# Deformable-convolution samples blended and scaled in their gather buffers instead of small buffers of their own

## The chip, the cores and the metric

The kernel runs on one core of a Trainium2 chip. The metric is the device time of one execution in microseconds (us), as the median of several executions of the same program. Five engines work beside each other, each through its own instructions in a fixed order: TensorE (PE; its weight loads are listed as PEld), VectorE (DVE), ScalarE (ACT), GpSimd (POOL), which here issues indirect DMAs, and SyncE (SP), which issues plain DMAs. They wait for each other through semaphores.

## The reference

One metaformer layer on `x` of shape 4 x 256 x 64 x 64 (images, channels, rows, columns), all in fp32. First three modulated deformable 3x3 convolutions, each followed by a ReLU, on the input normalised over channels; the result is added to `x`. Then a mixture of 8 experts (256 to 512 to 256, exact GELU), of which each position uses its best two, added again. The part that the change touches is the sampling of a deformable convolution:

```python
om = conv3x3(x, w_off) + b_off            # 27 channels: 9 offsets (dy, dx), 9 masks
ys = row + ky - 1 + dy                    # sampling place of each of the 9 taps
xs = col + kx - 1 + dx
sampled = bilinear(x, ys, xs) * sigmoid(mask)   # four neighbours, weighted
out = einsum('bikhw,oik->bohw', sampled, w) + b
```

## The kernel before

A layer of one image is a stage; there are 12 stages (3 layers, 4 images), ordered so that images interleave. A stage has 8 blocks of 512 positions (8 image rows), a block has 9 taps, and a tap has 4 tiles of 128 positions. One such tile of one tap is called a sample here: 128 positions x 256 channels. There are 12 x 8 x 9 x 4 = 3456 samples, handled in 1728 pairs.

The layer's input lies in HBM as a table whose rows hold a position and the one below it; two table rows that follow each other are two columns of the image. So one indirect DMA on POOL (L503) brings for each of 128 positions all four neighbours: 4 KB a partition, 512 KB in all, into a buffer `g` of the pool `gat`, which has `GB = 10` buffers (L38, L147). Then for each sample:

- L509, the column blend, on VectorE: in both columns the lower neighbour times its coefficient plus the upper, in place in `g` (512 elements a partition);
- L514, the row blend, on VectorE: the right column's result times its coefficient plus the left one's, into a small buffer `s` of the pool `smp` with 8 buffers (256 elements a partition);
- L517, the scaling by mask and weights, on ScalarE, in place in `s`.

`turn` handles a pair, two pairs behind the newest (`LAG = 2`): four 128x128 transposes on TensorE (L532) into PSUM, and a copy on ScalarE (L535) into `sT`. When the four samples of a tap are there, `finish` multiplies the preceding tap's `sT` with the tap's weights (L555: four matmuls of 128x512, each shown as two records) into the accumulator of the block; after nine taps ScalarE adds the bias and applies the ReLU (L577).

Other work is woven in, spread over the taps by the program: the offset convolution (L357) and sampling plan (L366 to L427) of coming blocks, the transposes and normalisation of coming images (L442 to L467), the storing of tables (L325 to L338), and the expert network of images that are done: its gathers on POOL (L800, L812, L915), matmuls on TensorE (L856, L874), GELUs on ScalarE (L866), and VectorE's bias and weighted sums (L892, L930). Expert gathers are queued behind the newest sample gather (`self.gathered`), and much of the VectorE work behind the newest row blend (`self.last`), with `self.after`, which fixes the order of issue on one engine and adds no wait.

The order in which each engine gets its instructions is set when the program is built, by a scheduler that works with its own estimates of durations and with the number of buffers in each pool; the chip then follows that order. A buffer that is handed on makes its next writer wait for the last reader of the old contents.

Of the kernel before, what the change touches and what calls it, by code (L numbers as in the profile page):

```python
# [8 lines left out]
F32 = mybir.dt.float32  # L9
I32 = mybir.dt.int32  # L10
AF = mybir.ActivationFunctionType
ALU = mybir.AluOpType
AX = mybir.AxisListType

P = 128
H = W = 64
C = 256
# [17 lines left out]
FT_LOG = 8  # L35
FT = 1 << FT_LOG
FU = FT // P
GB = 10  # L38
LAG = 2
LEAST = 2.0**-30  # L40
WINN = CC * (RPB + 2) * W
# [41 lines left out]
class Group:  # L83


    def __init__(self, b, n0, n1):
        self.b, self.n0, self.n1 = b, n0, n1
        self.nm = f"{b}_{n0}"
        self.M = (n1 - n0) * TPB

        self.NF = 2 * self.M * P // FT + E - 1


        self.half = (self.NF + 1) // 2
        self.zt, self.acc, self.gy, self.sums, self.py = {}, [], [], [], None
        self.order = [s // 2 + s % 2 * self.half for s in range(self.NF)]
# [21 lines left out]
class Weave:  # L118
# [3 lines left out]
    def __init__(self, ctx, tc, ins, out):  # L122
        nc = self.nc = tc.nc
        self.tc = tc
        self.ins = ins
        self.x = ins["x"].rearrange("b (c p) h w -> b p c (h w)", p=P)
        self.out_v = out.rearrange("b (c p) h w -> b p c (h w)", p=P)
        self.B = self.x.shape[0]

        def pool(name, bufs, **kw):  # L130
            return ctx.enter_context(tc.tile_pool(name=name, bufs=bufs, **kw))

        self.cst = pool("cst", 1)
        self.dram = pool("dram", 1, space=bass.MemoryType.DRAM)
        self.wkp = pool("wkp", 1)
        self.plan = pool("plan", 19)
        self.win = pool("win", 3)
        self.wt = pool("wt", 2)
        self.small = pool("small", 1)
        self.big = pool("big", 2)  # L140
        self.ffn = pool("ffn", 2)
        self.rt = pool("rt", 1)
        self.rt2 = pool("rt2", 2)
        self.gyp = pool("gyp", 4)
        self.smT = pool("smT", 2)
        self.smp = pool("smp", 8)
        self.gat = pool("gat", GB)  # L147
        self.ps = pool("ps", 3, space=bass.MemoryType.PSUM)
        self.ps1 = pool("ps1", 1, space=bass.MemoryType.PSUM)

        self.routes, self.tiles, self.sums = Lane(), Lane(), Lane()
        self.side, self.plans_side = [], []
        self.last = self.gathered = self.turned = None
        self.starting, self.draining, self.later = True, False, []
        self.pend, self.pairs = None, []
# [338 lines left out]
    def samples(self, i, n, k, t0, plan):  # L494


        nc = self.nc
        idx, cf = plan
        ss = []
        for t in (t0, t0 + 1):  # L500
            j = t * K + k
            g = self.gat.tile([P, 2, 2, C], F32, tag="g", name=f"g_{i}_{n}_{j}")
            self.gathered = nc.gpsimd.indirect_dma_start(  # L503
                out=g.rearrange("p x s f -> p (x s f)"),
                out_offset=None,
                in_=self.table(*self.stages[i]),
                in_offset=bass.IndirectOffsetOnAxis(ap=idx[:, j : j + 1], axis=0),
            )
            nc.vector.scalar_tensor_tensor(  # L509
                g[:, :, 0, :], g[:, :, 1, :], cf[:, j, 0:1], g[:, :, 0, :],  # L510
                ALU.mult, ALU.add,
            )
            s = self.smp.tile([P, C], F32, tag="s", name=f"s_{i}_{n}_{j}")
            self.last = nc.vector.scalar_tensor_tensor(  # L514
                s, g[:, 1, 0, :], cf[:, j, 1:2], g[:, 0, 0, :], ALU.mult, ALU.add
            )
            nc.scalar.activation(s, s, AF.Copy, scale=cf[:, j, 2:3])  # L517
            ss.append(s)
        return ss
# [616 lines left out]
```

## Time and profile before

| | |
|---|---|
| median of 9 runs | 7644.26 us (7624.54 to 7658.29) |
| profiled execution, its own time | 7608.72 us |
| its span, first to last instruction | 7607.0 us |
| mean granted TensorE clock | 0.94 |
| busy share of the span: TensorE, VectorE, ScalarE, POOL | 85%, 65%, 43%, 59% |
| DMA queue of the indirect gathers | 1947 MB, 72.5% of 16 DMA engines' span |
| 3456 gathers (L503) | 1069 ns each on POOL, 2435 us of POOL's idle time ahead of them |
| 3456 column blends (L509) | 743 ns each |
| 3456 row blends (L514) | 483 ns each |
| 3456 scalings (L517) | 508 ns each |
| 1728 copies of transposes (L535) | 586 ns each, 2409 us of ScalarE's idle time ahead of them |

In the profile's lists of groups a line has the source line, the engine, the operation, what is written and read with its shape, and the count; then, after a bar, the busy time in us and the mean of one instruction in ns; then, after a second bar, the engine's idle time just ahead of these instructions and what ended most of it. In the list of waits a line says who waited for whom: us in total, times, and the longest wait. "Issue" is time in which an engine waited for nothing that the profile shows, "remote" a wait whose end the profile could not attribute. In the timeline a line has the start and the duration in us, the engine, the line, the operation and the count, and in brackets the idle time ahead of it. Matmul ends are modelled in the records, so that TensorE's busy share isn't how close it is to its peak.

### The profile page before, as it was taken

The numbers are of one execution on the slowest core, as the hardware profiler recorded it, in microseconds if no ns is written. First come the engines' busy times: TensorE is split into PE (matmuls) and PEld (weight loads), VectorE is DVE, ScalarE is ACT, GpSimd is POOL, SyncE is SP. The second block draws the span as 40 slices with busy tenths as digits, with TensorE's granted clock in tenths as the row PEclk, the third lists the DMA queues.
The fourth block names the chain that finished last, engine by engine and source line by source line (L and its number), as shares of the span: only waits on it lengthen the run. The fifth ranks groups of instructions, "written<-read, shape, count | busy, mean of one in ns | idle before, by whom it ended". The sixth has DMA issues, their size and how long they took to land.

```text
span 7607.0 us, 88985 instructions
## 1 busy us (share of the span) xinstructions
PE 6459.0 (85%) x26500; PEld 3626.5 (48%) x26500; DVE 4952.9 (65%) x11467; ACT 3268.5 (43%) x7141; POOL 4485.9 (59%) x4245
## 2 busy tenths in 40 slices
PE   7897888888898888888987879988888788977887
PEld 3443333334444444455554445444444455644565
DVE  6776777768987666567777556656768454667421
ACT  3444444445544444445443434444444333444322
POOL 4654666656666556556557656655556565656543
PEclk8999999999999999999999989999999899999898
DMA  8997999989999888889888878888888777888644
GB/s 268 333 321 264 352 331 337 338 331 356 363 343 318 297 296 306 283 303 327 300 290 314 282 266 313 301 298 287 304 289 293 244 264 241 288 286 297 203 141 123
DMA packets 800319, 2223.73 MB, mean 292 GB/s; under 512 B 104728, under 2 KB 302872, under 8 KB 794080
## 3 DMA queue, kind: packets, MB, share of 16 engines
q0 software_dynamic: 551200, 1947.35, 72.5%
q1 hardware_dynamic: 248640, 270.69, 10.7%
q8 instruction: 215, 3.52, 0.2%
q14 instruction: 264, 2.16, 0.1%
HBM read 2160.68 MB, written 196.40 MB: 310 GB/s over the span
## 4 chain that ended last, share of the span: by engine, by line
PE 68%; ACT 10%; issue 8%; another core or an unknown queue 7%; DVE 4%; DMA 2%; POOL 1%; SPq 0%; ACTq 0%; POOLq 0%; DVEq 0%
PE acc L555 33%; PE tp L532 10%; PE ph L856 7%; PE py L874 7%; PE po L357 6%; ACT sT L535 3%; ACT s L517 3%; DVE g L509 1%; DVE s L514 1%; PE pm L371 1%; ACT hT L866 1%; ACT win L577 1%; PE ftp L840 1%; PE lp_tok L618 1%
## 5 line engine op out<-in xcount | busy, mean ns | idle before, releaser
L503 POOL DMA_INDIRECT g<-tab,idx x3456 | 3696.1, 1069 | 2435.4 <-DVE s L514 1095.6
L555 PE MATMUL acc<-sT,wk 128*128 128x512 f32 x6912 | 3501.5, 621 | 276.4 <-ACT sT L535 157.6
L509 DVE SCALAR_TENSOR_TENSOR g<-g,cf 128x512 f32<-128x512 f32 x3456 | 2560.8, 743 | 260.8 <-DMA g<-tab,idx 239.8
L514 DVE SCALAR_TENSOR_TENSOR s<-g,cf 128x256 f32<-128x256 f32 x3456 | 1663.2, 483 | 1394.2 <-PE tp L532 751.1
L535 ACT COPY sT<-tp 128x512 f32<-128x512 f32 x1728 | 1003.4, 586 | 2408.5 <-PE tp L532 1599.0
L555 PEld LDWEIGHTS acc<-sT,wk 128*128 128x128 f32 x6912 | 1201.3, 198 | 1128.5 <-issue 823.8
L517 ACT ACTIVATE s<-s,cf 128x256 f32<-128x256 f32 x3456 | 1631.1, 508 | 236.0 <-DVE s L514 145.0
L532 PEld LDWEIGHTS tp<-ident,s 128*128 128x128 f32 x6912 | 895.6, 146 | 1697.6 <-issue 999.9
L532 PE MATMUL tp<-ident,s 128*128 128x128 f32 x6912 | 1290.4, 287 | 461.5 <-ACT s L517 223.6
L856 PE MATMUL ph<-fzT,w 128*128 128x256 f32 x2608 | 720.3, 411 | 80.2 <-ACT fzT L844 30.1
L874 PE MATMUL py<-w,hT 128*128 128x256 f32 x2608 | 675.2, 397 | 120.1 <-ACT hT L866 66.2
L856 PEld LDWEIGHTS ph<-fzT,w 128*128 128x128 f32 x2608 | 507.1, 205 | 217.4 <-issue 80.1
L874 PEld LDWEIGHTS py<-w,hT 128*128 128x128 f32 x2608 | 485.5, 196 | 262.1 <-ACT hT L866 101.6
L866 ACT ACTIVATE hT<-ph,w 128x256 f32<-128x256 f32 x652 | 282.5, 472 | 619.2 <-PE ph L856 361.3
L812 POOL DMA_INDIRECT zt<-z,tok x326 | 335.3, 1028 | 159.5 <-issue 88.6
L800 POOL DMA_INDIRECT w<-in_W,wrow x163 | 176.2, 1081 | 400.3 <-ACT sT L535 163.3
L357 PE MATMUL po<-win,wo 128*32 128x504 f32 (+1 forms) x2304 | 364.3, 609 | 6.0 <-ACT win L301 3.6
L892 DVE TENSOR_TENSOR y<-py,w 128x512 f32<-128x512 f32 x163 | 111.9, 687 | 360.8 <-PE py L874 293.6
L915 POOL DMA_INDIRECT gy<-ys,slots x256 | 254.7, 995 | 104.8 <-issue 73.0
L930 DVE SCALAR_TENSOR_TENSOR ta<-gy,cw,ta 128x256 f32<-128x256 f32 x256 | 120.8, 481 | 121.3 <-DMA gy<-ys,slots 76.8
L357 PE MATMUL po<-win_pre,wo 128*32 128x504 f32 (+1 forms) x1152 | 185.7, 622 | 2.0 <-ACT om L366 2.0
L366 ACT ACTIVATE om<-po,bo 128x512 f32<-128x512 f32 x96 | 66.0, 688 | 247.1 <-PE po L357 155.9
(154 smaller groups left out, 2965.9 us busy)
## 6 DMA issues: line engine op xcount, KB each, us to landing
tab<-hv SPq DMA_DIRECT2D x512, 128.0 KB
g<-tab,idx POOLq DMA_INDIRECT x3456
ys<-y SPq DMA_DIRECT2D x163, 256.0 KB
tab<-h_pre SPq DMA_DIRECT2D x128, 256.0 KB
wk<-in_conv_w SPq DMA_DIRECT2D x99, 256.0 KB
xc_pre<-in_x SPq DMA_DIRECT2D x32, 512.0 KB
xr_tok<-in_x SPq DMA_DIRECT2D x32, 512.0 KB
t<-t_tok SPq DMA_DIRECT2D x32, 512.0 KB
```

What stands on the lines that cost most here:

```text
L357: nc.tensor.matmul(po[g * Q : (g + 1) * Q, :].rearrange("q (r w) -> q r w", w=W)[:, :, x0:x1], lhsT=self.wo[l][:, 3 * ky + kx, c, :], rhs= ...
L503: self.gathered = nc.gpsimd.indirect_dma_start(out=g.rearrange("p x s f -> p (x s f)"), out_offset=None, in_=self.table(*self.stages[i]), ...
L509: nc.vector.scalar_tensor_tensor(g[:, :, 0, :], g[:, :, 1, :], cf[:, j, 0:1], g[:, :, 0, :], ALU.mult, ALU.add,)
L514: self.last = nc.vector.scalar_tensor_tensor(s, g[:, 1, 0, :], cf[:, j, 1:2], g[:, 0, 0, :], ALU.mult, ALU.add)
L517: nc.scalar.activation(s, s, AF.Copy, scale=cf[:, j, 2:3])
L532: self.turned = nc.tensor.transpose(tp[:, c, u * P : (u + 1) * P], ss[u][:, c * P : (c + 1) * P], self.ident)
L535: nc.scalar.copy(self.sT[:, :, t0 * P : (t0 + 2) * P], tp)
L555: nc.tensor.matmul(acc[:, o, :], lhsT=self.wk[k][:, c, o * P : (o + 1) * P], rhs=sT[:, c, :], start=(k == 0 and c == 0), stop=(k == K - 1 ...
L812: self.nc.gpsimd.indirect_dma_start(out=zt, out_offset=None, in_=grp.zd, in_offset=bass.IndirectOffsetOnAxis(ap=grp.tok[:, j : j + 1], axi ...
L856: nc.tensor.matmul(ph[:, h, :], lhsT=w1[:, o : o + P], rhs=zT[:, c, :], start=(c == 0), stop=(c == CC - 1),)
L866: nc.scalar.activation(ht[:, h, :], ph[:, h, :], AF.Gelu, bias=w1[:, k : k + 1])
L874: nc.tensor.matmul(py[:, u, :], lhsT=hT[h // 2][:, h % 2, u * P : (u + 1) * P], rhs=w2[:, h * C : (h + 1) * C], start=(h == 0), stop=(h == ...
```

## The change

The pool `smp` of small buffers goes; the row blend writes its result over the first of its two inputs, in the gather buffer itself, and the scaling and the transposes work there. The pool of gather buffers grows from 10 to 13. In SBUF that is 13 x 4 KB in place of 10 x 4 KB + 8 x 1 KB a partition. A gather buffer is free for the next gather once the sample is transposed; before, once its row blend was done. Second, the code of a pair issues both gathers and both column blends first, and then both row blends, queued behind the second column blend. The arithmetic stays the same. The scheduler places the instructions anew.

```diff
-GB = 10
+GB = 13
...
-        self.smp = pool("smp", 8)
         self.gat = pool("gat", GB)
...
-        ss = []
+        ss, gs = [], []
         for t in (t0, t0 + 1):
             j = t * K + k
             g = self.gat.tile([P, 2, 2, C], F32, tag="g", name=f"g_{i}_{n}_{j}")
...
-            nc.vector.scalar_tensor_tensor(
+            newest = nc.vector.scalar_tensor_tensor(
                 g[:, :, 0, :], g[:, :, 1, :], cf[:, j, 0:1], g[:, :, 0, :],
                 ALU.mult, ALU.add,
             )
-            s = self.smp.tile([P, C], F32, tag="s", name=f"s_{i}_{n}_{j}")
-            self.last = nc.vector.scalar_tensor_tensor(
-                s, g[:, 1, 0, :], cf[:, j, 1:2], g[:, 0, 0, :], ALU.mult, ALU.add
-            )
+            gs.append((j, g))
+        for j, g in gs:
+            s = g[:, 0, 0, :]
+            with self.after(newest):
+                self.last = nc.vector.scalar_tensor_tensor(
+                    s, g[:, 1, 0, :], cf[:, j, 1:2], s, ALU.mult, ALU.add
+                )
             nc.scalar.activation(s, s, AF.Copy, scale=cf[:, j, 2:3])
             ss.append(s)
         return ss
```

## The prediction

> **What bounds the kernel now.** I read the page first, then the list of waits, then a short stretch of the timeline, and last the single records, matched sample by sample.
>
> ```profile
> span 7607.0 us, 88985 instructions
> ...
> PE 6459.0 (85%) x26500; PEld 3626.5 (48%) x26500; DVE 4952.9 (65%) x11467; ACT 3268.5 (43%) x7141; POOL 4485.9 (59%) x4245
> ...
> PE 68%; ACT 10%; issue 8%; another core or an unknown queue 7%; DVE 4%; DMA 2%; POOL 1%; SPq 0%; ACTq 0%; POOLq 0%; DVEq 0%
> ...
> L514 DVE SCALAR_TENSOR_TENSOR s<-g,cf 128x256 f32<-128x256 f32 x3456 | 1663.2, 483 | 1394.2 <-PE tp L532 751.1
> L535 ACT COPY sT<-tp 128x512 f32<-128x512 f32 x1728 | 1003.4, 586 | 2408.5 <-PE tp L532 1599.0
> ```
>
> TensorE ends last: 68% of the chain. VectorE, whose queue the change reorders, holds only 4% of it (some 300 us), although it sits idle 1394 us ahead of its row blends.
>
> ```profile
> ACT sT L535 <- PE tp L532: 1599.0, 933, 5.9
> POOL g L503 <- DVE s L514: 1095.6, 634, 15.2
> ...
> DVE s L514 <- PE tp L532: 751.1, 625, 8.8
> PEld tp L532 <- ACT s L517: 554.9, 849, 8.6
> ...
> ACT s L517 <- DVE s L514: 145.0, 150, 4.3
> ```
>
> The second and third rows are what the change removes: a gather waits for a buffer that a row blend frees, a row blend for a small buffer that a transpose frees. But TensorE itself waits for ScalarE's scaling (fourth row), and ScalarE waits for the blends only 145 us in the whole run. Between them lies a round trip, seen here:
>
> ```profile
> 2002.66 0.60 PE L532 MATMUL tp<-ident,s 128*128 128x128 f32 x4
> ...
> 2003.30 0.59 ACT L535 COPY sT<-tp 128x512 f32<-128x512 f32 x1 [1.57 <-PE tp L532]
> 2003.78 0.51 ACT L517 ACTIVATE s<-s,cf 128x256 f32<-128x256 f32 x1
> ...
> 2004.31 0.50 ACT L517 ACTIVATE s<-s,cf 128x256 f32<-128x256 f32 x1
> ```
>
> ScalarE copies a pair's transposes out, and only then scales the next pair, which TensorE needs next. Over all records the steps are steady: start of the last transpose to start of the copy 0.309 us, copy to first scaling 0.482, first to second scaling 0.410, second scaling 0.510 long, then 0.053 to the transpose. With the last transpose's own 0.109 that is 1.87 us a pair. Start to start, a transpose takes 0.109 us and a tap's 128x512 record 0.429 (two records a matmul), so four transposes and two matmuls fill 2.15 us and cover it; with one matmul between, TensorE idles about 0.58 us.
>
> So TensorE is not full: by such start-to-start times its work is about 5.8 ms of the 7.6. Just ahead of transposes it idles about 730 us, ahead of tap matmuls 530 us. For 303 transposes (359 us) the late scaling stood directly behind the copy on ScalarE; a late row blend explains only some 10 us.
>
> **Part 1: 18 places become 13.** The k-th record of L503, L509, L514, L517 and the k-th pair of L532 belong to one sample, in both kernels. Medians for a sample before: issue to landing 6.05 us (landing read from its completion events), landed until the column blend 9.2, row blend until scaling 9.7, scaled until transposed 1.2; 29.5 in all, at one sample every 2.2 us. So it spends some 20 us waiting in one buffer or another. Now gather k must wait for the transposes of k-13. I pushed each gather's issue to that moment (at least 1.27 us behind the one before, as the trace spaces them, more where FFN fetches stand between), kept its own landing time, and compared with the slack that the sample had. The median slack falls from 21 to 14 us; 14 of 3456 samples come too late, by 39 us added up. Late neighbours share their lateness, so I take +10 us, bounds 0 and 39. Ten places would give 79 late samples and 164 us. FFN weights and rows, queued behind gathers on POOL, slip as much as the gather ahead of them; none that I could match was late by this count.
>
> **Part 2: VectorE no longer waits for transposes.** The 751 us go, and most of the 249 listed as remote ahead of the same line. What is late next is the landing: a column blend can't start before the transposes of k-13 plus some 6.3 us, the row blend at some 7.8 us, that is 3.5 samples, so VectorE runs at most some 9.5 samples ahead of TensorE where it ran 8. In the new order no row blend stands directly behind its own column blend (2380 did). Such a row blend started 0.133 us after the column blend's end; the 82 behind another sample's started 0.081 us before it. So up to 2380 x 0.214 = 509 us of VectorE time go.
>
> [...]
>
> What this is worth to the end is bounded by those who wait for VectorE: ScalarE for blends 145.0 + 31.3 us; TensorE for the other VectorE work that queues behind blends: normalised rows for L462 40.6 + 29.3, routing matrices L783 23.0 + 41.1, sums L948 27.3 + 21.1. Together 359 us, the largest gain. The blends' part hardly reaches TensorE (the 10 us above): I take 15. Of the other 182 I take a quarter, 45, since most of it is the work's own length. Sum -60; the loss side is 0, as no VectorE step gets longer.
>
> **Part 3: the scheduler's order.** The built programs differ little on POOL (0.5% of instructions moved) and SP (1.5%), but pairs move on ScalarE and TensorE. Pairs whose four transposes stand together rise from 657 to 1398 of 1728; before, a tap matmul often stood between the halves. Transpose copies with no scaled sample queued ahead of them rise from 1230 to 1474, those with just one fall from 261 to 6, those with two or more stay (237, 248). I laid the steady steps above along both orders, with row durations for all else, and added up where TensorE has too little to cover the round trip. Before: 238 us ahead of transposes, 192 ahead of taps. After: 190 and 240. Both 430: I take 0. It explains a third of the measured idle, so the bounds are wide. The best: pairs of each pattern of transposes and matmuls cost after what that pattern costs in the trace before (4 transposes then 3 matmuls: 346 ns idle in 21 cases, split around one matmul: 700 ns in 196); this gives 1377 us instead of 1588, -211. The worst: each of the 244 additional copies without a sample ahead costs the difference in TensorE idle within 4 us between none ahead (1126 ns) and two (455): +164.
>
> **Part 4: more semaphore instructions.** A sample's buffer now carries waits of its gather's queue to ScalarE and TensorE. Waiting instructions ahead of L517 rise from 218 to 3469 (17 ns each), ahead of L532 from 1454 to 3415 (51 ns). They wait for what came long ago. A scaling behind a copy starts 0.105 us before its end with such an instruction (68 cases) as without (1333), a transpose behind a tap record 0.429 us after its start either way. I take 0; exposed, it would be 55 + 100 us. The scaling's and transposes' own work stays equal, as does that of the blends.
>
> **Sum.** The profiled execution took 7608.72 us (span 7607.0 and 1.7 around it): +10 - 60 + 0 + 0 gives 7559. The median of the nine runs, 7644.26, lies 0.47% above it; so 7594.
>
> **Rivals.**
> - Slower: ScalarE's queue becomes more serial. In 85% of pairs, not 71%, the scaling stands behind the copy that waits for TensorE. For it: the idle by number ahead, 1126 against 455 ns, and that 554.9 us already end with a scaling. Against: the added-up round trips are equal. From about 75 of the 244 copies on (50 / 0.67) it eats the gain; in full it gives 7608.72 + 164 - 50, scaled 7759.
> - No change: TensorE and ScalarE pace each other, VectorE's waits were slack. For it: VectorE's 4% of the chain and the 10 us. Then 7644, within 0.2%, about what a measurement of this kernel can tell from no change.
> - Large gain: the closed-up transposes bring the full -211, in all -261: 7382. Against: the patterns that become frequent are rare before (21 cases).
> - The 13 places bind: as if there were ten, +164 less 60, 7749. Against: 14 us of median slack left.
>
> **How the numbers follow.** Forecast of a small gain (0.2 to 1.5%) 0.35, large gain 0.12, no change 0.13, serial ScalarE or binding places 0.40 (0.31 and 0.09), most of it well short of its full price. Faster 0.47, same 0.13, slower 0.40. The range runs from 7470, half of the large gain, to 7750, most of the slower cases. The likeliest case alone: 7530 to 7629.
>
> **What would show it.** Right: the wait of L514's row blend for L532 gone, POOL's wait for a buffer now ended by L532 or L517's lines, samples still landing well ahead of their column blend, TensorE's idle ahead of transposes and taps within 100 us of 1260. Wrong: column blends waiting several hundred us for gathers (places bind), the waits of transposes for scalings up by over 100 us (serial ScalarE), or idle down by 200 (order).

## Result and profile after

The changed kernel took 7550.31 us (median of 10 runs, 7518.67 to 7567.24) against 7637.48 us for the kernel before in 31 runs of the same measurement: ratio 0.9882, 95% interval 0.9866 to 0.9898. It is faster by 87 us, 1.2%, where 50 us, 0.7%, was forecast. The profiled execution took 7556.55 us (7608.72 before). On another chip the same change made the kernel slower by 1.2%. So the forecast has the sign of this chip, little more than half the size, and, as the runs below show, a wrong reason: that the sign came out right was luck.

The page of the changed kernel:

```profile
span 7554.6 us, 94248 instructions
...
PE 6447.7 (85%) x26500; PEld 3630.1 (48%) x26500; DVE 4849.7 (64%) x11467; ACT 3255.4 (43%) x7141; POOL 4725.7 (63%) x4245
...
L508 DVE SCALAR_TENSOR_TENSOR g<-g,cf 128x512 f32<-128x512 f32 x3456 | 2560.5, 748 | 1710.1 <-DMA g<-tab,idx 1253.1
L537 ACT COPY sT<-tp 128x512 f32<-128x512 f32 x1728 | 1001.2, 585 | 2498.1 <-PE tp L534 1558.4
...
L516 DVE SCALAR_TENSOR_TENSOR g<-g,cf 128x256 f32<-128x256 f32 x3456 | 1527.2, 479 | 1.1 <-DVE g L508 0.9
```

The row blend (L516, before L514) had 1394 us of idle time ahead of it and now has 1.1. The idle time went to the column blend (L508), mostly for landings: 1710 us now, 261 before:

```profile
L509 DVE SCALAR_TENSOR_TENSOR g<-g,cf 128x512 f32<-128x512 f32 x3456 | 2560.8, 743 | 260.8 <-DMA g<-tab,idx 239.8
```

VectorE's busy time fell by 103 us, but the span fell by 52, so VectorE stands idle 51 us longer than before. The page's chain of waits can't be set beside that of before: it breaks off some 220 us before the end.

The list of waits of the changed kernel:

```profile
ACT sT L537 <- PE tp L534: 1558.4, 956, 7.0
DVE g L508 <- DMA g<-tab,idx: 1253.1, 953, 10.5
...
POOL g L502 <- PE tp L534: 776.5, 466, 8.8
...
PEld tp L534 <- ACT g L519: 559.6, 610, 10.1
ACT sT L537 <- remote: 530.5, 124, 12.1
...
ACT g L519 <- DVE g L516: 128.8, 90, 11.6
```

The gathers' wait for a buffer, 1096 us before (for row blends), is now 776.5 for transposes, with 232.8 more that copies end and 150.1 that scalings end. The transposes' wait for scalings is where it was (554.9 before). Counted from start to start, TensorE's idle time ahead of transposes went from 729 to 691 us, of tap matmuls from 534 to 659, of the expert matmuls (L858, L876) from 356 to 227. This count gives each record its usual step as work, so the total, 2299 to 2247, must fall by as much as the span; only the places tell something. Its level is too high: it takes in steps at half clock (0.853 us for a tap record in place of 0.429), and it counts most of the offset convolution, whose records start side by side (2327 of 3178 steps in the trace before are under 20 ns), as idle (some 400 us, as in every kernel here).

One row doesn't fit a kernel paced by its buffers: "remote", 530.5 us in 124 copies, up to 12.1 us each. This is one of them, in the timeline of the changed kernel (weight loads left out, and gathers, which went on):

```profile
2242.77 0.60 PE L534 MATMUL tp<-ident,g 128*128 128x128 f32 x4
...
2243.21 1.02 PE L557 MATMUL acc<-sT,wk 128*128 128x512 f32 x2
...
2248.20 0.58 ACT L537 COPY sT<-tp 128x512 f32<-128x512 f32 x1 [5.58 <-remote]
...
2248.68 0.91 ACT L519 ACTIVATE g<-g,cf 128x256 f32<-128x256 f32 x2
2249.25 0.69 PE L534 MATMUL tp<-ident,g 128*128 128x128 f32 x2 [5.01 <-issue]
```

The copy needs the four transposes that start at 2242.77. Elsewhere it starts 0.31 us after the last of them; here 5 us pass, in which TensorE starts two tap records and then nothing. I call this a late stretch. I counted them from the single records: wherever a copy, GELU or other reader on ScalarE or VectorE had waited and began more than 1.2 us after the last TensorE record that it reads had started, the time between, less 0.4 us, overlaps merged. The kernel before has 304 such readers and 885 us of late stretches, the changed one 330 and 916. A wider rule, with every GELU counted, gives 80 to 120 us more for each trace that has late stretches and puts them in nearly the same order.

### The profile page after: what moved, and what is told of

It reads as the page before. It is cut to its first block, busy times and chain, and to the rows that moved or that the text cites. A ratio compares the mean times of both kernels' runs of the same rounds, so it can differ in the third digit from the quotient of the medians.

```text
span 7554.6 us, 94248 instructions
## 1 busy us (share of the span) xinstructions
PE 6447.7 (85%) x26500; PEld 3630.1 (48%) x26500; DVE 4849.7 (64%) x11467; ACT 3255.4 (43%) x7141; POOL 4725.7 (63%) x4245
## 5 line engine op out<-in xcount | busy, mean ns | idle before, releaser
L502 POOL DMA_INDIRECT g<-tab,idx x3456 | 3867.7, 1119 | 2181.1 <-PE tp L534 776.5
L508 DVE SCALAR_TENSOR_TENSOR g<-g,cf 128x512 f32<-128x512 f32 x3456 | 2560.5, 748 | 1710.1 <-DMA g<-tab,idx 1253.1
L557 PEld LDWEIGHTS acc<-sT,wk 128*128 128x128 f32 x6912 | 1237.8, 199 | 1439.7 <-issue 1123.9
L519 ACT ACTIVATE g<-g,cf 128x256 f32<-128x256 f32 x3456 | 1570.0, 506 | 192.0 <-DVE g L516 128.8
L534 PE MATMUL tp<-ident,g 128*128 128x128 f32 x6912 | 1174.4, 285 | 436.2 <-ACT g L519 289.2
L516 DVE SCALAR_TENSOR_TENSOR g<-g,cf 128x256 f32<-128x256 f32 x3456 | 1527.2, 479 | 1.1 <-DVE g L508 0.9
L534 PEld LDWEIGHTS tp<-ident,g 128*128 128x128 f32 x6912 | 845.4, 145 | 1329.6 <-issue 659.3
L858 PE MATMUL ph<-fzT,w 128*128 128x256 f32 x2608 | 674.3, 396 | 54.0 <-ACT hT L868 19.7
L876 PE MATMUL py<-w,hT 128*128 128x256 f32 x2608 | 660.4, 394 | 68.6 <-ACT hT L868 32.4
L858 PEld LDWEIGHTS ph<-fzT,w 128*128 128x128 f32 x2608 | 503.2, 199 | 227.6 <-issue 99.9
L876 PEld LDWEIGHTS py<-w,hT 128*128 128x128 f32 x2608 | 489.5, 196 | 204.6 <-issue 77.2
L814 POOL DMA_INDIRECT zt<-z,tok x326 | 369.4, 1133 | 173.6 <-issue 85.4
L356 PEld LDWEIGHTS po<-win,wo 128*32 128x32 f32 x2304 | 75.5, 113 | 245.0 <-issue 192.3
```

The costliest lines, as they stand in the source:

```text
L356: nc.tensor.matmul(po[g * Q : (g + 1) * Q, :].rearrange("q (r w) -> q r w", w=W)[:, :, x0:x1], lhsT=self.wo[l][:, 3 * ky + kx, c, :], rhs= ...
L502: self.gathered = nc.gpsimd.indirect_dma_start(out=g.rearrange("p x s f -> p (x s f)"), out_offset=None, in_=self.table(*self.stages[i]), ...
L508: newest = nc.vector.scalar_tensor_tensor(g[:, :, 0, :], g[:, :, 1, :], cf[:, j, 0:1], g[:, :, 0, :], ALU.mult, ALU.add,)
L516: self.last = nc.vector.scalar_tensor_tensor(s, g[:, 1, 0, :], cf[:, j, 1:2], s, ALU.mult, ALU.add)
L534: self.turned = nc.tensor.transpose(tp[:, c, u * P : (u + 1) * P], ss[u][:, c * P : (c + 1) * P], self.ident)
L557: nc.tensor.matmul(acc[:, o, :], lhsT=self.wk[k][:, c, o * P : (o + 1) * P], rhs=sT[:, c, :], start=(k == 0 and c == 0), stop=(k == K - 1 ...
```

## Experiments

My theory after the result: the gain is VectorE's freedom, since a row blend no longer waits for a small buffer. The rivals: it comes from the pair order, or from something that only this chip has. Measurements are told apart by their chips; each ratio is against the kernel before, measured beside it on the same chip. The chip of the result itself is not on record.

**The halves, ten places, and more small buffers (chip 4, before 6807.56 us).** `pairs_only` keeps the buffers of before and takes only the pair order, the second half of the change's diff. `inplace_only` takes only the buffers:

```diff
-GB = 10
+GB = 13
...
-        self.smp = pool("smp", 8)
...
-            s = self.smp.tile([P, C], F32, tag="s", name=f"s_{i}_{n}_{j}")
+            s = g[:, 0, 0, :]
             self.last = nc.vector.scalar_tensor_tensor(
-                s, g[:, 1, 0, :], cf[:, j, 1:2], g[:, 0, 0, :], ALU.mult, ALU.add
+                s, g[:, 1, 0, :], cf[:, j, 1:2], s, ALU.mult, ALU.add
             )
```

`inplace10` is the changed kernel with `GB = 10`; `smp12` is the kernel before with `pool("smp", 12)`.

`pairs_only`:


> The pair order alone: column blends of a pair ahead of its row blends, but 10 gather buffers and 8 small ones as before. The built order of TensorE and ScalarE is nearly that of the changed kernel (pairs with closed-up transposes 1396 of 1728, copies with no scaled sample ahead 1441). Theory O (the gain comes with the order of the pair, through the order on TensorE and ScalarE): 0.986 to 0.991 of before, near the change's 0.988, and VectorE still waits some 750 us for transposes ahead of row blends. Theory B (the gain comes from VectorE no longer waiting for small buffers): 0.998 to 1.004.

`inplace_only`:


> The buffers alone: blended, scaled and transposed in 13 gather buffers, but each sample's row blend stands right behind its own column blend, as before. The built order is nearly that of before (642 closed-up pairs, 1250 copies with none ahead). Theory B: 0.986 to 0.991, with the wait of row blends for transposes gone. Theory O: 0.998 to 1.003 although that wait is gone. If the two halves add up, this run and the pair order alone multiply to 0.988.

`inplace10`:


> The changed kernel with 10 gather buffers in place of 13; its built order is nearly the same (1410 closed-up pairs). By the prediction's count of late gathers, 10 places would make 79 samples late by 164 us in sum against 39 us at 13, so 30 to 130 us slower than the changed kernel: 0.992 to 1.005 of before. If 13 already bind, the step from 13 to 10 is much larger, over 200 us: above 1.015. If places never bind here: 0.987 to 0.990.

`smp12`:


> Before with 12 small buffers in place of 8 (the same bytes as 13 gather buffers), everything else as before; built order nearly unchanged (664 closed-up pairs). Row blends then wait much less for transposes. Theory B: most of the gain, 0.988 to 0.994. Theory O: 0.998 to 1.002, with the wait of row blends for transposes cut to under half of its 751 us.

Measured: pairs_only 6852.3 us, ratio 1.0069 (1.0057 to 1.0081); inplace_only 6834.44, 1.0046 (1.0034 to 1.0058); inplace10 6966.92, 1.0242 (1.0229 to 1.0255); smp12 6805.24, 0.9999 (0.9990 to 1.0007).

The kernel before was 830 us faster here than in the result, and neither half gained. 12 small buffers did nothing. None of these four traces has more than one late reader.

**The same halves where the kernel before takes 7.5 ms (chip 10, before 7506.56 us).** The change itself and its halves:

> The changed kernel itself, unaltered, beside its two halves on one chip. In its first profile and in that of before, TensorE's work sometimes completes late: the copy of a pair starts over 1 us after the start of its last transpose 182 times before and 230 times after, some 700 us in sum, and each kernel takes 7.6 ms; in the profiles of the halves this never happens, and before took 6807.56 us beside them. Theory S (the change gains only where such stalls are frequent): 1.000 to 1.012 where before takes some 6.8 ms, about 0.988 where it takes some 7.6 ms. Theory O+B (the halves multiply): 1.0115 at 6.8 ms. Theory G (the change gains everywhere): 0.986 to 0.991 at either.

> The pair order alone, beside the changed kernel. Where before takes some 6.8 ms: 1.007 as in the first run. Where it takes some 7.6 ms, theory S with the gain in the order: 0.988 to 0.993; with the gain in the buffers: 0.998 to 1.007.

> The buffers alone, beside the changed kernel. Where before takes some 6.8 ms: 1.0046 as in the first run. Where it takes some 7.6 ms, theory S with the gain in the buffers, since VectorE no longer stands still through a TensorE stall: 0.988 to 0.993; with the gain in the order: 0.998 to 1.005.

Measured: the change 7447.28 us, 0.9928 (0.9906 to 0.9951); pair order alone 7564.92, 1.0095 (1.0070 to 1.0120); buffers alone 7360.72, 0.9811 (0.9784 to 0.9838). The gain is the buffers', and the pair order takes about 1% back: buffers and order together stand to buffers alone as 7447.28 to 7360.72, 1.012. All three traces have late stretches, 942 us with the pair order alone, 659 with the buffers alone, 808 with both.

**The change where nothing is late (chip 0, before 6805.27 us).** With a profile of the kernel before on this chip:

> Before itself, unaltered, for a profile on the chip of this call. Theory S counts stretches in which a consumer starts over 1.2 us after the start of the TensorE instruction it waits for: some 880 us in sum where it takes 7.5 to 7.6 ms (first profile 885 us), under 30 us where it takes some 6.8 ms. If the whole difference between the two kinds of chip is these stretches, the span less their sum is 6.7 to 6.8 ms on both.

> The changed kernel again, unaltered. Theory S: 0.986 to 0.995 if before takes 7.5 to 7.6 ms here, 1.003 to 1.015 if it takes some 6.8 ms (the halves there: 1.0069 and 1.0046). Theory G: under 0.995 on either.

> Before with 12 small buffers in place of 8. Where before takes some 6.8 ms: 0.9999 as in the first run. Where it takes 7.5 to 7.6 ms: if the buffers help because VectorE isn't held up through a late transpose (theory B), 0.980 to 0.990, near the buffers-alone kernel's 0.9811; if they help because TensorE reads its samples from other places or through other waits, so that its late stretches get fewer (theory L), 0.997 to 1.003 and late stretches as in before.

> The buffers alone again, beside the two. Where before takes 7.5 to 7.6 ms: 0.978 to 0.985 with late stretches of some 660 us against some 880 us of before (theory L), or late stretches equal to those of before and a shorter rest (theory B). Where before takes 6.8 ms: 1.0046.

Measured: before 6801.39 us; the change 6882.23, 1.0122 (1.0106 to 1.0137); smp12 6807.0, 1.0003 (0.9993 to 1.0012); buffers alone 6835.6, 1.0052 (1.0037 to 1.0067). The change is slower, by the product of its halves (1.0069 x 1.0046 = 1.012).

The list of waits of the kernel before, on this chip:

```profile
ACT sT L535 <- PE tp L532: 1823.0, 1176, 5.4
POOL g L503 <- DVE s L514: 662.4, 553, 14.0
PEld acc L555 <- issue: 657.7, 2666, 0.8
...
DVE s L514 <- PE tp L532: 466.7, 540, 4.9
...
ACT s L517 <- DVE s L514: 416.5, 398, 8.9
DVE g L509 <- DMA g<-tab,idx: 403.4, 282, 10.4
```

Beside it, the same kernel on chip 13 (below), 7505.6 us:

```profile
POOL g L503 <- DVE s L514: 1050.1, 642, 14.6
...
PEld acc L555 <- issue: 811.7, 2781, 10.2
...
DVE s L514 <- PE tp L532: 710.1, 610, 12.1
...
ACT sT L535 <- remote: 357.3, 93, 10.5
...
DVE g L509 <- DMA g<-tab,idx: 239.2, 89, 10.6
```

The last column tells the two kinds of chip apart at a glance: a tap's weight load waits at most 0.8 us for "issue" on the one, 10.2 on the other, and "remote" copies exist only on the other. Row blends wait 467 us, not 710, and gathers 662, not 1050: a third of the two waits that the change removes is there only with late stretches. And column blends already wait 403 us for landings.

Two rows of the pair order alone (chip 4) and two of the whole change (chip 0):

```profile
DVE g L509 <- DMA g<-tab,idx: 920.5, 759, 11.7
...
ACT s L520 <- DVE s L517: 465.4, 344, 11.8
```

```profile
DVE g L508 <- DMA g<-tab,idx: 1129.1, 1043, 10.6
...
ACT g L519 <- DVE g L516: 507.7, 362, 11.0
```

Landings come later than VectorE wants them, and ScalarE waits longer for its row blend: 417, 465 and 508 us in before, pair order and change. Against the kernel before the span is 49.5 us longer with the pair order (chip 4), 31 with the buffers and 79 with the change. TensorE's idle time rises ahead of transposes (393, 443, 417 and 461 us in before, pair order, buffers and change) and, with the pair order, of taps (314, 356, 314, 363); the pair order takes back some 67 us ahead of expert matmuls.

The records tell what held up the transposes. Where TensorE idled ahead of one whose scaling ended less than 0.4 us earlier, that scaling mostly had either started right behind a row blend that ended last, or stood behind a transpose copy on ScalarE. Behind late row blends TensorE idled 45 us in before, 121 with the pair order, 71 with the buffers, 137 with the change, and 27 with 12 small buffers; behind copies 136, 115, 137, 117 and 134. With the pair order 118 of the 158 late row blends had a column blend of their pair that started within 0.3 us of its landing. So ahead of transposes the loss on these chips is late row blends, mostly behind late landings, and not a more serial ScalarE.

**What the buffers gain from late stretches (chip 13, before 7512.31 us).** VectorE's freedom should show with 12 small buffers, if it is the reason. `inplace10c` is inplace_only with `GB = 10`.

> The kernel before with 12 small buffers in place of 8, all else as before. Where TensorE's completions come late (the kernel before at 7500 to 7650 us): theory B says that the buffers half gains because VectorE's row blend, with 8 small buffers, stands still while a late stretch holds the transposes, so 12 buffers should bring much of the gain of the buffers alone (ratio 0.980 to 0.990, wait of row blends for transposes from some 750 us to under 400). Theory L says that the gain comes from the stretches themselves, which are fewer or shorter when the scalings and transposes work in the gather buffers (659 us of them against 885 to 942 in three other runs); then 12 small buffers give 0.997 to 1.003 and the stretches stay near 900 us. Where nothing is late (before at 6800 to 6810 us) both say 1.000, as measured twice, and nothing is told apart.

> The buffers alone: 13 gather buffers worked in place, each row blend right behind its own column blend. Where TensorE's completions come late: 0.978 to 0.985 by both theories (0.9811 measured before); theory L expects its late stretches to add up to 600 to 720 us again, theory B expects 850 to 950 and takes the 659 us of the other run for chance. Where nothing is late: 1.0035 to 1.0055, as measured twice.

> The buffers alone, in place, but with 10 gather buffers in place of 13. Each gather then waits for the transposes of the tenth sample back. Where nothing is late: the 13-to-10 step cost the changed kernel 1.2% and should cost this one as much, so 1.012 to 1.020. Where completions come late, theory B expects VectorE's room ahead of TensorE to be no more than in the kernel before (some 6 to 7 samples), so no gain is left: 1.000 to 1.015; theory L expects fewer late stretches still, so 0.99 to 1.000.

> The kernel before, for its profile on the same chip. Late copies behind transposes: 850 to 950 us of late stretches where its time is 7500 us or more, under 30 us where it is 6800.

Measured: smp12 7750.94 us, 1.0339 (1.0314 to 1.0364); buffers alone 7384.18, 0.9836 (0.9812 to 0.9861); buffers alone with ten places 7395.33, 0.9866 (0.9826 to 0.9905); before 7507.28. My theory isn't borne out: with 12 small buffers the row blends' wait for transposes goes from 710 to 532 us, and the kernel loses 3.4%. That is less relief than was expected (under 400 us), and late stretches lie over it. Its waits have longer "issue":

```profile
PEld acc L555 <- issue: 853.8, 2800, 16.7
...
DVE s L514 <- PE tp L532: 531.6, 478, 8.2
```

And ten places in place, no more than before, still gain. In these four kernels the time goes with the sum of the late stretches (all in us, one trace of each):

| chip 13 | span | readers late | late stretches | span less these | at half clock |
|---|---|---|---|---|---|
| before | 7505.6 | 300 | 806 | 6700 | 837 |
| smp12 | 7749.2 | 292 | 987 | 6762 | 1081 |
| buffers alone, 13 | 7374.7 | 254 | 664 | 6711 | 664 |
| buffers alone, 10 | 7371.8 | 235 | 604 | 6768 | 654 |

Buffers alone: 142 us fewer of them for a span 131 shorter. Ten places: 202 fewer, and 68 lost elsewhere. smp12: 181 more for a span 244 longer.

The kernels with the pair order don't fit this sum. In the result's own two traces the stretches rise from 885 to 916 us while the span falls, so that the span less these goes from 6722 to 6639; on chip 10 it is 6661 with the change and 6605 with the pair order alone, against 6735 with the buffers alone. So fewer stretches can't be what made the change itself faster in the result, and no run shows by which mechanism it became so.

**Is it the in-place work, or any small change (chip 13, before now 7638.45 us)?** `swapped` declares `gat` ahead of `smp`, so that both lie elsewhere in SBUF and no instruction moves; `smp10` has 10 small buffers, `gat11` 11 gather buffers and the 8 small ones.

```diff
-        self.smp = pool("smp", 8)
         self.gat = pool("gat", GB)
+        self.smp = pool("smp", 8)
```

> The kernel before with its two pools declared in the other order: the small buffers then lie behind the gather buffers in SBUF, and every engine's instructions stay the same, in the same order. Where nothing is late (before at 6800 us): 1.000. Where TensorE's completions come late (before at 7500 us or more): if the stretches hang on the order of the instructions, 0.997 to 1.003, 800 to 950 us of stretches, at the places where the kernel before has them (84% of its places came back in a second run, 23% by chance); if they hang on where the operands lie in SBUF, the places change and the ratio may go anywhere from 0.98 to 1.03.

> The kernel before with 10 small buffers in place of 8; the built order changes in some 300 lines of TensorE. Where nothing is late: 1.000. Where completions come late: if more small buffers bring the stretches (12 of them gave 987 us of stretches against 806, ratio 1.034), some 1.015; if a neutral change of the program is enough to move the stretches by chance, anything from 0.97 to 1.03.

> The kernel before with 11 gather buffers in place of 10, small buffers kept. Where nothing is late: 0.997 to 1.001. Where completions come late: if what gained was the in-place work alone, 0.995 to 1.005 and 800 to 950 us of stretches; if a neutral change of the program moves the stretches by chance, anything from 0.97 to 1.03.

Measured: swapped 7637.46 us, 0.9999 (0.9983 to 1.0016), 883 us of late stretches; smp10 7685.07, 1.0061 (1.0039 to 1.0083), 923; gat11 7633.17, 0.9995 (0.9979 to 1.0011), 902. With the two pools at other addresses (swapped) the stretches add up to much the same (883 us, against 885 and 806 in the first trace of before and in that on chip 13), so here they don't hang on these addresses. They come back where they were: of the places (by tap matmul, within four records) where the first profile of before has one, 84% have one in the profile of before on chip 13 and 85% in swapped, 60% in smp10, 39% with the buffers alone, 23% by chance. So they go with the order of instructions, on these chips. Two nearly neutral changes moved the time by 0.6% and less; the buffers alone gained 1.9 and 1.6%. smp12 shows that a kernel that isn't in place can be moved far, too: its span was 244 us longer, with 181 us more of stretches. So the two kernels with the buffers alone have fewer stretches in three runs, on chip 13 beside the kernel before and on chip 10 (659 us) against its traces from elsewhere, as none was taken there. That in-place work must bring this, and why, isn't shown; 13 gather buffers with the small ones kept were not run.

## Why the prediction was right and wrong

**Part 2 (VectorE, -60)** is the step that failed: it is the only part of the sum with a gain, and the runs don't show that gain. It took the row blends' 751 us as pacing by small buffers, gave 15 us for the blends and a quarter of what else waits for VectorE, 45. Where nothing is late, smp12 takes away 177 of the 467 us that row blends wait, in its list of waits on chip 0:

```profile
DVE s L514 <- PE tp L532: 290.1, 339, 5.1
```

It was worth nothing, ratio 0.9999 and 1.0003; where stretches are late, it came with a loss of 3.4%. More small buffers gained in none of the four runs (smp10 is the fourth), and the buffers alone, which end this wait, lose 0.5% where nothing is late. What gained is a term that the sum doesn't have: the in-place buffers alone gain 128 and 146 us by the medians on chips 13 and 10, where late stretches exist, and have fewer of them. The stretches were in the trace before, in the rows "remote" and "issue" with a longest wait of 10 us and more, two of them here; I read their sums and not their lengths.

```profile
PEld acc L555 <- issue: 823.8, 2788, 10.3
...
ACT sT L535 <- remote: 440.8, 103, 14.1
```

How the change, whose stretches aren't fewer in the result, gains 87 us stays open; by the halves it is what the buffers gain less what the pair order costs.

Part 2 also left out a wait that the pair order adds: the first sample's row blend now stands behind the second sample's column blend, and so behind the second landing. So "the loss side is 0" was wrong. The closed gap is real: with the pair order alone VectorE was busy 4814.9 us, with the order of before on chip 0 4963.0, at the same 11467 instructions; in the trace after, the 1510 row blends that stand directly behind a column blend, always another sample's, start 0.083 us before its end (median). But the 0.214 us are not of one piece: 2324 row blends, at a median of 0.133 us, had an instruction ahead that waits for the small buffer, and the 56 without one started 0.035 us after their column blend's end. So I estimate that 0.12 us (0.035 + 0.081) go with a sample's own column blend just ahead, and the other 0.10 (0.133 - 0.035) with the waiting instruction. Yet ScalarE's wait for row blends rose from 417 to 465 us, and the kernel lost 0.7 to 1.0%.

**Part 3 (order, 0)** and the pair order's wait come with the same half, which cost 0.7% (45 us by the medians, chip 4) and 0.95% (58 us by the medians, chip 10) measured alone; the change against its buffers alone gives 0.7% and 1.2%. Ahead of transposes the records of chip 4 tell them apart: idle time behind late row blends rose by 76 us, behind copies it fell by 21, where Part 3 had 238 go to 190. Ahead of taps the idle time rose by 42, where Part 3 had 192 go to 240; that this is the order wasn't followed back. So Part 3 was near, and the wait that Part 2 left out is the larger loss where nothing is late. In the result's traces late row blends rose only from 16 to 32 us. The built order follows the pairing and hardly the buffers: copies with no scaled sample ahead are 1230 before, 1441 with the pair order alone, 1250 with the buffers alone, 1474 with both.

**Part 1 (places, +10)** used the slack of a chip with late stretches. There it held roughly: ten and thirteen places in place differ by no more than their intervals. Where nothing is late, 13 to 10 places cost 1.2% (1.0242 over 1.0122, some 82 us), half of the 164 that ten places were given and inside the 30 to 130 that were expected of the step; the two ratios are from two chips. Of the slack the first half went: a landed sample lay 9.2 us before its column blend in the trace before, 0.6 after. The second half stayed, between row blend and scaling 9.7 us before and 8.5 after (all medians). So VectorE waits for landings, and few transposes do.

**Part 4 (semaphore instructions, 0)**: the buffers alone, which have these instructions (94315 in all, as the change 94248), lose 0.5% where nothing is late, some 30 us with their places. Late row blends ahead of transposes make up 27 of these (45 to 71 above). So little is left for the semaphore instructions, far from the 155 of full exposure.

**What would show it.** The wait for L532 went, POOL's wait is ended by transposes and scalings, idle ahead of transposes and taps is 1350 us, within 100 of 1260: as said. Samples landing well ahead of their column blend: no. Column blends waiting several hundred us for gathers, the sign for the rival of binding places, came (1253 us), and without its price on this chip. The serial ScalarE's sign, transposes waiting 100 us longer for scalings, did not come (554.9 to 559.6, with TensorE's own row for the same wait 778.5 to 848.8). The small gain of the forecast is, on chip 0, a loss of 77 us; the large gain's cause, closed-up transposes, is the half that loses.

**What beats both kernels.** Buffers alone, without the pair order: 0.9811 (chip 10) and 0.9836 (chip 13), against 0.9928 (chip 10) and 0.9882 (the result) for the change. On chips 4 and 0 nothing that was run beats the kernel before; 12 small buffers equal it.

## What to carry to other kernels

Before a wait is priced, look at its longest case beside its sum, and at rows without a releaser: here the weight loads of the taps waited for "issue" 811.7 us on chip 13 (2781 times, 0.3 us on average, the longest 10.2) and 657.7 us on chip 0 (the longest 0.8), so that the longest wait, more than the sum, told of the late stretches. Relieving VectorE's wait for small buffers gained nothing here (12 of them: 0.9999, 1.0003 and 1.0339), and an issue order that makes a sample wait for its neighbour's landing cost more than the closed gaps brought (1.0069 and 1.0095). A gain of a per cent should be measured on more than one chip (the change here: 0.9882, 0.9928 and 1.0122); halves of a change, run alone, told at once which part carried it and where.

## What the runs showed of the hardware

The same program takes 6.80 ms on chips 0 and 4 and 7.51 to 7.64 ms on chips 10 and 13, and on chip 13 it moved from 7512 to 7638 us between two measurements. The difference is largely in some 300 late readers of TensorE's results, with stretches mostly of 1 to 10 us, 604 to 987 us in all, against one reader and 16 to 18 us in each of the eight traces of chips 0 and 4. Where they fall goes with the program's order of instructions (84% of the places come back in another run of it), and whether they come goes with the chip.

The late stretches and the half-speed clock of TensorE go together. The clock is at half for 654 to 1081 us in the four traces of the table above, and for 292 to 389 us in those of chips 0 and 4; from start to start a tap record takes 0.853 us there, 0.429 elsewhere. In the first trace of the kernel before, at half clock for 917 us, only 12 of the 182 late copies fall inside a half-clock stretch, but of the 141 half-clock stretches 101 begin within 10 us after a late stretch (by the wider rule) began; 43 would by chance. Of the 141, 73 last 3.41 us and 67 a multiple of it; one lasts 50.09. By this order in time half clock looks like a consequence of the late stretches and not their cause; what switches the clock isn't shown.

What starts a stretch stays open. Instruction fetches don't go with them: in the trace before, one of either fetch queue falls into a stretch or the microsecond ahead of it in 9% and 11% of the cases (12% and 15% by chance). The places show no period in TensorE's count of instructions, from 16 to 4096 of them, and exchanging the SBUF addresses of the two pools left them where they were.
